# The fill of an attention stage: the chain's slices take precedence over scores, in banks of their own, with rows written from other queues

## The chip, the core and the metric

The kernel runs on one core of one Trainium2 chip. Times are device microseconds (us) of a whole execution. The engines are PE (TensorE; PEld is its weight load), DVE (VectorE), ACT (ScalarE), POOL (GpSimd) and SP (SyncE, which here only issues DMAs). Each engine works through its own instructions in order and waits for others at semaphores.

## What is computed

The reference is a stack of four "macaron" blocks on 2048 rows of 128 numbers, in float32. Each block is half a feed-forward step, attention (or a long convolution), and another half feed-forward step, each on a layernorm of the rows and added to them. The change bears on the last two blocks:

```python
x = x + 0.5 * _L2_ffn_ref(_layernorm(x), ...)   # gate, up, down: 128 -> 384 -> 128
x = x + _L2_attn_ref(_layernorm(x), ...)        # 16 heads of 8, rotary
x = x + 0.5 * _L2_ffn_ref(_layernorm(x), ...)
x = x + 0.5 * _L3_ffn_ref(x, ...)               # gated attention of 16 heads, then experts
x = x + _L3_attn_ref(_layernorm(x), ...)        # 16 heads of 8, rotary, causal
x = x + 0.5 * _L3_ffn_ref(x, ...)
```

So there are four attentions of 16 heads: L2's own (here rope2), that within the first L3 feed-forward step (gated0), L3's own (rope3, causal) and that within the second L3 feed-forward step (gated1).

## The kernel before, in words

**Tiles.** The 2048 rows are four chunks (`NC`) of 512 (`CW`), each four tiles (`TC`) of 128. Keys of all heads lie in `kp`, 128 partitions x 8 pairs of heads x 2048, in a high and a low part with rows of constants between them (ones, `one_rows`), so that a score and the subtraction of its maximum are one matmul. A query unit is one chunk and one group of four heads, (qc, g); `qps` are four buffers for units, with a constant filling of zeros. Two rows of such a buffer take minus the maxima (`h_mT`). Values are in `va`.

**An attention** is the function `attend`. It walks through half-steps: a score step (matmuls `sn` into a bank pair of pool `sc`, two of them, then the DVE reduction `h_mx`) and a weight step (matmuls `st` into pool `tp`, three banks, an exponential on ACT to `pr`, and the products with values, `av`). A unit's weights need all of its maxima: when its last score is out, `maxima` (L1018 on) forms `h_m`, `h_mr`, `h_mt` on DVE, transposes them on PE (`mt_ps`), copies them on ACT (`h_mT`) and writes four DMAs into `qp`.

**Modes.** `order["mode"]` is "fill" while no weight has been issued, "core" from the first weight, and "drain" when the scores are those of the next attention. In fill the attention has nothing but scores of unit 0 (and then of unit 1) and what it is still missing: the chain `carried`, with the last chunk's feed-forward step (`l2_chunk` for rope2: norm, matmuls `gu`, `hid`, `po`, sum into x) and then `prepare` (norm, transposes `xn_tp`, projection `pj`, rotation `rot` with the tables `cos` and `sin`, high and low part, and for keys `spread` into `kp` from on chip, `keys_here`). Beside it runs `own`, with values of all chunks and queries 1 to 3. In each step of the loop both of these are given one slice, so slices and scores alternate.

**What sets the order.** `pin` keeps a PE instruction in program order when `order["pinned"]` is set: scores and weights always, slices in all modes but fill. DVE work of class `Ordered` is kept in order in core, drain and host. What is not kept in order is placed by a scheduler. Buffers of `banks()`, such as `pj` and `gu`, come in fill from pool `sc`, the same as the scores'.

**Keys.** The first three chunks of rope2's keys were written to DRAM (`dk`) during the stage before. `attend` loads them by SP at its start (`load_keys`, in two halves of four pairs, 24 DMAs of 128 KB). Ahead of a load the constants of all rows must be in `kp`: `constant_rows` for pairs 0 to 3 in `head_buffers`, for 4 to 7 in `other_rows()`, called between the halves. Pairs with p % 4 < 2 are written by ACT (L1538), the others by DVE (L1540); `qps` 0 by DVE and 1 to 3 by POOL (L1544), followed by the memset of `va` (L1549).

Of the kernel before, what the change touches and what calls it, by code (L numbers as in the profile page):

```python
# [2 lines left out]

# [1 line left out]

# [6 lines left out]
F32 = mybir.dt.float32  # L12
# [4 lines left out]
ALU = mybir.AluOpType  # L17
# [4 lines left out]
P = 128  # L22
# [3 lines left out]
CW = 512  # L26
NC = S // CW
# [3 lines left out]
HD = 8  # L31
NG = 4
PARK = 2
NEG = -1.0e30
NK = 32
KD = 64
# [7 lines left out]
def tile_macaron(ctx: ExitStack, tc: tile.TileContext, a: dict, out: bass.AP):  # L44
    nc = tc.nc
# [23 lines left out]
    order = {"pinned": False, "mode": "free"}  # L69
# [23 lines left out]
    def transpose(dst, src):  # L93
        pin(nc.tensor.transpose(dst, src, ident))  # L94
# [3 lines left out]
    pools = {"keep": ctx.enter_context(tc.tile_pool(name="keep", bufs=1))}  # L98
# [28 lines left out]
    one_rows = const.tile([P, 1], F32, name="one_rows")  # L127
# [556 lines left out]
            return self.tiles[key[1]][key[0], key[2]]  # L684

    def banks(name):
        if order["mode"] == "host":
            return TwoBanks(name)
        return pools["sc"].tile([P, 2, CW], F32, tag="sc", name=name)

# [17 lines left out]
    def chain(tasks):  # L708
        for task in tasks:
            yield from task  # L710
            yield 1
# [52 lines left out]
    class Heads:  # L764
# [3 lines left out]
        def __init__(self):  # L768
            self.current = False
            self.queries = {}  # L770
            self.units = [(qc, g) for qc in range(NC) for g in range(NG)]
            self.scores, self.weights = [], []
            for u in self.units:
                nk = u[0] + 1 if self.causal else NC
                nkb = (u[0] + 1) * TC if self.causal else NT
                if u == self.units[0]:
                    self.scores += [(self, u, t, kc) for kc in range(nk) for t in range(TC)]
                else:
                    self.scores += [(self, u, t, kc) for t in range(TC) for kc in range(nk)]
                self.weights += [(u, kb) for kb in range(nkb)]  # L780
            self.scored = 0
            self.waiting_keys, self.loaded, self.sent, self.valued, self.ready = [], set(), set(), set(), set()


# [2 lines left out]
        def keys_here(self, c):  # L787
            cs = slice(c * CW, (c + 1) * CW)
            hi, lo = (kp[:, 2 * PARK + n, cs] for n in range(2))
            yield from self.project("k", c, hi, lo)  # L790
# [32 lines left out]
            yield 1  # L823


        def load_keys(self, c, halves=(0, 1)):
            for h in halves:
                ps = slice(4 * h, 4 * h + 4)
                for j in range(2):
                    for n in range(2):  # L830
                        r = j * KD + n * 2 * HD
                        nc.sync.dma_start(
                            out=kp[r : r + 2 * HD, ps, c * CW : (c + 1) * CW].bitcast(F32),
                            in_=rows_of(dk[c], j)[:, ps, :],
                        )
            self.loaded.update((c, h) for h in halves)
# [137 lines left out]
    def attend(A, carried, follow, after=None):  # L974
# [6 lines left out]
        def begin(B, u):  # L981
            qc, g = u
            assert qc in B.sent
            qp = qps[turn["qp"] % len(qps)]
            turn["qp"] += 1
            for j in range(2):
                nc.sync.dma_start(
                    out=qp[j * KD : j * KD + KR + 2, :, :].bitcast(F32),
                    in_=rows_of(dq[qc], j)[:, 2 * g : 2 * g + 2, :],
                )  # L990
            mx = small.tile([P, TC, 4, NC], F32, tag="h_mx", name="h_mx")
            B.queries[u] = qp, mx

        def score(B, u, t, kc, p):
            qc, g = u
            qp, mx = B.queries[u]
            diag = B.causal and kc == qc
            wd = (t + 1) * P if diag else CW
            sc = banks("sn")
            for j in range(2):  # L1000
                r = slice(j * KD, (j + 1) * KD)
                pin(nc.tensor.matmul(  # L1002
                    sc[:, j, :wd], lhsT=qp[r, p, t * P : (t + 1) * P],
                    rhs=kp[r, 2 * g + p, kc * CW : kc * CW + wd], start=True, stop=True,
                ))
            if diag:
                vec.tensor_tensor(
                    sc[:, :, wd - P : wd], sc[:, :, wd - P : wd],
                    mask_qk.unsqueeze(1).to_broadcast([P, 2, P]), ALU.add,
                )  # L1010
            vec.tensor_reduce(mx[:, t, 2 * p : 2 * p + 2, kc], sc[:, :, :wd], AX.X, ALU.max)

        def maxima(u):
            qc, g = u
            qp, mx = queries[u]
            nk = qc + 1 if causal else NC
            m = small.tile([P, TC, 4], F32, tag="h_m", name="h_m")
            vec.tensor_reduce(m, mx[:, :, :, :nk], AX.X, ALU.max, negate=True)  # L1018
            mr = small.tile([P, TC, 4], F32R, tag="h_mr", name="h_mr")
            vec.tensor_copy(mr, m)  # L1020
            mt = small.tile([P, TC, 4, 2], F32, tag="h_mt", name="h_mt")
            vec.tensor_copy(mt[:, :, :, 0], mr.bitcast(F32))
            vec.tensor_tensor(mt[:, :, :, 1], m, mr.bitcast(F32), ALU.subtract)
            yield 1
            pt = bank("mt_ps")[0:8, :]
            for t in range(TC):
                transpose(
                    pt[:, t * P : (t + 1) * P], mt[:, t, :, :].rearrange("p s h -> p (s h)")
                )
            mT = small.tile([8, CW], F32R, tag="h_mT", name="h_mT")  # L1030
            nc.scalar.copy(mT, pt)  # L1031
            for s in range(4):
                r = (s % 2) * KD + KR
                nc.sync.dma_start(
                    out=qp[r : r + 2, s // 2, :].bitcast(F32), in_=mT[2 * s : 2 * s + 2, :].bitcast(F32)
                )

# [72 lines left out]

        if units[0] not in queries:
            begin(A, units[0])
        for h in range(2):
            for c, halves in A.waiting_keys:
                if h in halves:
                    A.load_keys(c, (h,))
            if h == 0 and A is rope2:
                other_rows()
        LAG = 4
        waiting = []  # L1120
        ready = {}
        last = None
        own = chain([A.value(c) for c in range(NC)] + [A.query(c) for c in range(1, NC)])
        beside = [[0, task] for task in (*carried, own)]
        followed = 0

        n = nw = 0
        while nw < len(weights) or last:
            order["pinned"] = True
            B = A if A.scored < len(A.scores) else after  # L1130
            s = B.scores[B.scored] if B and B.scored < len(B.scores) else None
            w = weights[nw] if nw < len(weights) else None
# [17 lines left out]
            k = units.index(s[1]) + 1 if s and B is A else len(units)  # L1150
# [11 lines left out]
            for _, task in due:  # L1162
                later = next(task, None)
                if later is not None:
                    waiting.append((n + later, task))
            if order["mode"] == "drain":
                while followed in finished:
                    beside.append([n, chain(follow(followed))])
                    followed += 1
            order["pinned"] = order["mode"] != "fill"  # L1170
            for entry in beside[:2]:
                if entry[0] <= n:
                    later = next(entry[1], None)
                    if later is None:
                        beside.remove(entry)
                    else:
                        entry[0] = n + later
# [348 lines left out]
    def head_buffers(pool):  # L1526
        kp = pool.tile([P, NH // 2, S], F32R, name="kp")
        va_flat = pool.tile([P, NT, NH * (HD + 1) + 32], F32, name="va")
        qps = [pool.tile([P, 2, CW], F32R, name=f"qp{k}") for k in range(4)]
        n = (NC - 1) * CW  # L1530


        def constant_rows(pairs):
            for p in pairs:
                dst = kp[:, p, 0:n].rearrange("p (t d) -> p t d", d=P)
                src = ones.unsqueeze(1).to_broadcast([P, n // P, P])
                if p % 4 < 2:
                    nc.scalar.activation(dst, src, AF.Identity, bias=one_rows, scale=0.0)  # L1538
                else:
                    nc.vector.tensor_scalar(dst, src, 0.0, one_rows, ALU.mult, ALU.add)  # L1540

        for k, qp in enumerate(qps):
            engine = nc.gpsimd if k else nc.vector
            engine.tensor_scalar(  # L1544
                qp.rearrange("p k (t d) -> p (k t) d", d=P), ones.unsqueeze(1).to_broadcast([P, 2 * TC, P]),
                0.0, None, ALU.mult,
            )
        constant_rows(range(4))
        nc.gpsimd.memset(va_flat, 1.0)  # L1549
        spread_w = pool.tile([P, 2, 2, P], F32R, name="spread_w")  # L1550
        return kp, va_flat, qps, spread_w, lambda: constant_rows(range(4, 8))

    with early:
# [4 lines left out]
        with tc.tile_pool(name="act1", bufs=1) as act:  # L1558
# [10 lines left out]
            rope2, rope3 = RopeHeads("l2", w2, False), RopeHeads("l3", w3, True)  # L1569
            l1_ffn(w1, [chain([l2_chunk(c, w2), rope2.prepare(c)]) for c in range(NC - 1)])  # L1570
    heads = ctx.enter_context(tc.tile_pool(name="heads", bufs=1))
    kp, va_flat, qps, spread_w, other_rows = head_buffers(heads)
# [134 lines left out]
```

## Time and profile before

| | us |
|---|---|
| runs (three) | 4069.31, 4070.45, 4085.0 |
| median | 4070.45 |
| profiled execution, its own time | 4069.46 |
| its span | 4067.7 |
| PE busy | 3575.4 (88%) |
| DVE busy | 3120.2 (77%) |
| ACT busy | 2378.7 (58%) |
| POOL busy | 279.1 (7%) |

The mean granted clock of TensorE was 0.888. The fills of the four attentions, found in the trace by the last x of the chain and the first `st`:

| attention | fill, about us | first norm's result on PE | first st |
|---|---|---|---|
| rope2 | 737 to 852 | 755.78 | 852.27 |
| gated0 | 1573 to 1665 | 1589.47 | 1665.23 |
| rope3 | 2505 to 2592 | | 2592.31 |
| gated1 | 3163 to 3210 | 3179.90 | 3209.87 |

Busy shares are averages over these fills and the long core and drain stages between, so they are read by stretches, as below. In a row of a view, "out<-in" names the tiles, "x4" the number of instructions, and an arrow in a wait points to what ended it.

### The profile page before, as it was taken

How to read it: one execution, taken by the hardware profiler on the slowest of the kernel's cores; microseconds unless marked ns; L12 is line 12 of the kernel's file. 1: busy time of each engine (PE TensorE's matmuls, PEld its weight loads, DVE VectorE, ACT ScalarE, POOL GpSimd, SP SyncE). 2: the span in 40 equal slices, each digit the busy share in tenths (PEclk: the TensorE clock that was granted, in tenths of full speed). 3: DMA queues.
4: the chain of work that ended last, by engine and by line, in shares of the span. 5: the costliest groups of instructions: out<-in, count | busy, mean ns of one | idle time of the engine just before them, and what ended most of it. 6: DMA issues, size and time to landing. Idle time of an engine off the chain costs nothing. (4 is left out here: it accounts for less than half of the span.)

```text
span 4067.7 us, 72222 instructions
## 1 busy us (share of the span) xinstructions
PE 3575.4 (88%) x29160; PEld 1695.2 (42%) x29160; DVE 3120.2 (77%) x5432; ACT 2378.7 (58%) x4515; POOL 279.1 (7%) x528
## 2 busy tenths in 40 slices
PE   8789899589999996899999965589997899999965
PEld 8556655333333342333333343233333333333334
DVE  2855354589999974799999845489996799999844
ACT  1222133168888862688888722246675588888732
POOL 2000011210000000000000023100000000000013
PEclk9889799789999997899999966578897899999965
DMA  2100000210000001100000022300002100000012
GB/s 71 24 1 1 1 16 27 52 53 7 10 7 10 5 12 42 35 7 10 7 10 5 9 63 76 97 24 11 10 2 57 44 10 7 10 7 7 7 46 71
DMA packets 63630, 98.96 MB, mean 24 GB/s; under 512 B 8656, under 2 KB 28864, under 8 KB 63040
## 3 DMA queue, kind: packets, MB, share of 16 engines
q1 hardware_dynamic: 54224, 70.86, 6.3%
q0 software_dynamic: 7728, 22.91, 2.1%
q8 instruction: 230, 3.77, 0.4%
q14 instruction: 104, 0.85, 0.1%
q10 hardware_dynamic: 1344, 0.57, 0.1%
HBM read 64.25 MB, written 29.00 MB: 23 GB/s over the span
## 5 line engine op out<-in xcount | busy, mean ns | idle before, releaser
L84 DVE TENSOR_REDUCE h_mx<-sn 128x2 f32<-128x1024 f32 (+1 forms) x1856 | 2204.6, 1197 | 133.9 <-PE sn L1002 111.9
L1058 ACT ACTIVATE pr<-st 128x512 f32<-128x512 f32 x3712 | 1971.3, 585 | 512.8 <-PE st L76 322.2
L76 PE MATMUL av<-pr,va 128*32 128x256 f32 x14592 | 1188.4, 398 | 10.8 <-ACT h_ot L1087 10.7
L76 PE MATMUL st<-qp,kp 64*128 64x512 f32 x3712 | 996.2, 499 | 43.9 <-ACT pr L1058 38.9
L1002 PE MATMUL sn<-kp,qp 64*128 64x512 f32 (+3 forms) x3712 | 804.9, 413 | 104.3 <-DMA qp<-dq 58.5
L76 PEld LDWEIGHTS st<-qp,kp 64*128 64x128 f32 x3712 | 394.7, 188 | 809.5 <-ACT pr L1058 427.7
L76 PEld LDWEIGHTS av<-pr,va 128*32 128x32 f32 x14592 | 292.6, 109 | 662.6 <-issue 625.5
L1002 PEld LDWEIGHTS sn<-kp,qp 64*128 64x128 f32 x3712 | 385.3, 194 | 165.3 <-issue 64.0
L614 ACT ACTIVATE hid<-h 128x512 f32<-128x512 f32 x128 | 76.2, 597 | 235.2 <-PE h L76 229.5
L84 DVE TENSOR_TENSOR hid<-hid,h 128x512 f32<-128x512 f32 x128 | 87.3, 686 | 114.3 <-PE h L76 102.3
L76 PEld LDWEIGHTS po<-w_l_w3T,hid 128*128 128x128 f32 x1024 | 126.5, 193 | 38.4 <-issue 28.0
L76 PE MATMUL po<-w_l_w3T,hid 128*128 128x128 f32 x1024 | 128.6, 278 | 4.8 <-DVE hid L84 4.7
L76 PE MATMUL h<-m_xc,w_l_w12T 128*128 128x512 f32 x256 | 128.5, 640 | 0.1
L1392 POOL DMA_INDIRECT wt<-in_b_wt,w_row_i x30 | 28.6, 953 | 1434.8 <-DVE slot_i L84 1387.3
L76 PE MATMUL h<-xnT,w_l_w12T 128*128 128x512 f32 x256 | 118.1, 604 | 0.4 <-DVE logits L594 0.4
L247 POOL TENSOR_TENSOR x<-x,w_b_n2b 128x512 f32<-128x512 f32 x8 | 10.1, 1266 | 1130.9 <-DVE rows L84 1127.4
L84 DVE BATCH_NORM_STATS2 st<-ph 128x6 f32<-128x256 f32 x46 | 19.9, 432 | 88.0 <-PE ph L76 88.0
L94 PE MATMUL xn_tp<-ident,xn_t 128*128 128x128 f32 x64 | 20.5, 401 | 75.2 <-ACT xn_t L213 71.7
L1031 ACT CAST h_mT<-mt_ps 8x512 fp32r<-8x512 f32 x64 | 36.8, 575 | 80.7 <-PE mt_ps L94 80.5
L84 DVE TENSOR_TENSOR st<-st,mask_kq 128x128 f32<-128x128 f32 x256 | 63.2, 290 | 17.6 <-PE st L76 16.8
L84 DVE TENSOR_TENSOR sn<-sn,mask_qk 128x256 f32<-128x256 f32 x128 | 54.0, 425 | 27.8 <-PE sn L1002 26.5
L76 PEld LDWEIGHTS h<-m_xc,w_l_w12T 128*128 128x128 f32 x256 | 50.3, 207 | 51.5 <-issue 48.2
(420 smaller groups left out, 2863.1 us busy)
## 6 DMA issues: line engine op xcount, KB each, us to landing
qp<-dq SPq DMA_DIRECT2D x128, 136.0 KB
kp<-dk SPq DMA_DIRECT2D x88, 128.0 KB
dq<-hi SPq DMA_DIRECT2D x32, 256.0 KB
dq<-lo SPq DMA_DIRECT2D x32, 256.0 KB
wt<-in_b_wt SPq DMA_DIRECT2D x16, 258.0 KB
qp<-h_mT SPq DMA_DIRECT2D x256, 4.0 KB
cos<-in_l_cos POOLq DMA_DIRECT2D x12, 256.0 KB, 4.0
sin<-in_l_sin POOLq DMA_DIRECT2D x12, 256.0 KB, 5.2
```

What stands on the lines that cost most here:

```text
L76: pin(nc.tensor.matmul(dst, lhsT=lhsT, rhs=rhs, start=start, stop=stop))
L84: ins = method(*args, **kw)
L94: pin(nc.tensor.transpose(dst, src, ident))
L247: nc.gpsimd.tensor_tensor(xs, xs, row.unsqueeze(1).to_broadcast([P, TC, D]), ALU.add)
L614: nc.scalar.activation(hid[:, hb, :], p_1, AF.Silu)
L1002: pin(nc.tensor.matmul(sc[:, j, :wd], lhsT=qp[r, p, t * P : (t + 1) * P], rhs=kp[r, 2 * g + p, kc * CW : kc * CW + wd], start=True, stop=True,
L1031: nc.scalar.copy(mT, pt)
L1058: nc.scalar.activation(pr[:, off:CW], sc[:, off:], AF.Exp, scale=A.scale)
L1392: nc.gpsimd.indirect_dma_start(wts[k], None, a["b3_wt"], bass.IndirectOffsetOnAxis(ap=w_row_i[:, s - E : s - E + 1], axis=0),)
```

## The change

- In fill, `banks()` gives two single banks of pool `tp`; scores take theirs from `sc` directly in all modes.
- In fill nothing on PE is kept in program order, scores included. A slice of the chain (not of `own`) is emitted at a higher priority (`AHEAD`, 2000) for the scheduler.
- Queries 1 to 3 leave `own` and become `asking`, started once all scores of unit 0 are out (`A.first`).
- The rows of maxima (`h_mT`) are written from POOL's queue in fill and from SP's otherwise.
- For rope2 the second halves of the keys (`late_keys`), with their constants (`other_rows()`), wait until the mode is no longer fill, and are loaded from POOL's queue.
- Constants: pairs 0 and 1 by ACT, 2 and 3 by DVE, 4 to 7 by POOL and kept in order; all four `qps` by DVE.

```diff
     def banks(name):
-        if order["mode"] == "host":
+        if order["mode"] in ("host", "fill"):
             return TwoBanks(name)
...
+            self.first = sum(score[1] == self.units[0] for score in self.scores)
...
-        def load_keys(self, c, halves=(0, 1)):
+        def load_keys(self, c, halves=(0, 1), queue=nc.sync):
...
-                        nc.sync.dma_start(
+                        queue.dma_start(
...
-            sc = banks("sn")
+            sc = pools["sc"].tile([P, 2, CW], F32, tag="sc", name="sn")
...
-                nc.sync.dma_start(
+                where = nc.gpsimd if order["mode"] == "fill" else nc.sync
+                where.dma_start(
                     out=qp[r : r + 2, s // 2, :].bitcast(F32), in_=mT[2 * s : 2 * s + 2, :].bitcast(F32)
                 )
...
+        late_keys = []
         for h in range(2):
             for c, halves in A.waiting_keys:
-                if h in halves:
+                if h and A is rope2:
+                    late_keys.append(c)
+                elif h in halves:
                     A.load_keys(c, (h,))
-            if h == 0 and A is rope2:
-                other_rows()
...
-        own = chain([A.value(c) for c in range(NC)] + [A.query(c) for c in range(1, NC)])
+        own = chain([A.value(c) for c in range(NC)])
+        asking = [chain([A.query(c) for c in range(1, NC)])]
...
-            order["pinned"] = True
+            order["pinned"] = nw > 0
...
-            order["pinned"] = order["mode"] != "fill"
+            if order["mode"] != "fill" and late_keys:
+                other_rows()
+                for c in late_keys:
+                    A.load_keys(c, (1,), nc.gpsimd)
+                late_keys.clear()
+            if asking and A.scored >= A.first:
+                beside.append([n, asking.pop()])
             for entry in beside[:2]:
                 if entry[0] <= n:
-                    later = next(entry[1], None)
+                    ahead = order["mode"] == "fill" and entry[1] is not own
+                    with tc.high_priority(offset=AHEAD) if ahead else nullcontext():
+                        later = next(entry[1], None)
...
-                if p % 4 < 2:
+                if p < 2:
                     nc.scalar.activation(dst, src, AF.Identity, bias=one_rows, scale=0.0)
+                elif p < 4:
+                    nc.vector.tensor_scalar(dst, src, 0.0, one_rows, ALU.mult, ALU.add)
                 else:
-                    nc.vector.tensor_scalar(dst, src, 0.0, one_rows, ALU.mult, ALU.add)
+                    tc.keep_in_program_order(
+                        nc.gpsimd.tensor_scalar(dst, src, 0.0, one_rows, ALU.mult, ALU.add)
+                    )
...
         for k, qp in enumerate(qps):
-            engine = nc.gpsimd if k else nc.vector
-            engine.tensor_scalar(
+            nc.vector.tensor_scalar(
                 qp.rearrange("p k (t d) -> p (k t) d", d=P), ones.unsqueeze(1).to_broadcast([P, 2 * TC, P]),
                 0.0, None, ALU.mult,
             )
```

More of the change, by code (lines that the diff above doesn't have):

```diff
@@ L1 @@
 import math
-from contextlib import ExitStack
+from contextlib import ExitStack, nullcontext
 import numpy as np
@@ L33 @@
 PARK = 2
+AHEAD = 2000
 NEG = -1.0e30
```

## The prediction

> **What bounds the kernel now.** I read the page's first part, then the engine windows, then the waits of one window, then single tiles. The first part says that PE is busy for 88% and DVE for 77%, which hides that the kernel has stages with different limits. The windows (busy us of each engine in a stretch, instructions in brackets, then the granted TensorE clock, DMA share, GB/s) tell them apart:
>
> ```profile
> 750.00:800.00 50.00, 30.34 (x96) 15.48 (x96) 27.89 (x33) 4.02 (x8) 3.96 (x17) 0.70 0.31 68
> 800.00:850.00 50.00, 34.00 (x86) 14.43 (x86) 30.48 (x42) 9.71 (x17) 15.78 (x28) 0.62 0.25 78
> 900.00:950.00 50.00, 49.76 (x484) 18.67 (x484) 49.01 (x47) 43.33 (x81) 0.00 (x0) 1.00 0.02 8
> 1600.00:1650.00 50.00, 37.17 (x128) 19.90 (x128) 20.65 (x30) 17.15 (x29) 4.04 (x15) 0.70 0.00 0
> 2540.00:2590.00 50.00, 13.72 (x55) 9.15 (x55) 19.26 (x44) 5.17 (x9) 11.28 (x23) 0.53 0.52 124
> ```
>
> In 900 to 950, a core stage, PE (49.76) and DVE (49.01) are both full at clock 1.00: nothing can be hidden there, and what stops DVE there is lost for good. The other four rows are fill stages: no engine is full and the clock is 0.53 to 0.70. There a chain of dependent steps sets the end. The waits of the first fill (rope2, 738 to 853) name it (total us waited, times, longest):
>
> ```profile
> POOL ln_h L185 <- DVE ln_g L84: 48.9, 2, 47.6
> ACT xn_t L213 <- POOL ln_nb L208: 27.1, 2, 21.4
> POOL rot L902 <- DVE rot L84: 22.8, 3, 10.0
> PEld xn_tp L94 <- ACT xn_t L213: 22.5, 6, 16.2
> PE xn_tp L94 <- ACT xn_t L213: 21.0, 2, 16.0
> DVE h_mx L84 <- PE sn L1002: 19.0, 6, 5.8
> DVE va L84 <- POOL va L1549: 4.0, 1, 4.0
> ```
>
> PE waits 16.0 us for the first norm, and POOL 47.6 for statistics that stand behind scores on DVE. The change works in these fills: rope2 about 115 us long, gated0 93, rope3 88, gated1 48. It can gain only there, and whatever it pushes out of a fill goes into a full core stage.
>
> **Rope2's fill, by steps.** Times are those of the profiled run. Two tiles price the constants (ns min/median/max, first and last start):
>
> ```profile
> L1544 POOL TENSOR_SCALAR qp<-ones x3: 3470/3471/3488, 737.3 to 744.2; 128x1024 fp32r<-128x1024 f32 x3
> L1544 DVE TENSOR_SCALAR qp<-ones x1: 680/680/680, 738.3 to 738.3; 128x1024 fp32r<-128x1024 f32 x1
> L1538 ACT ACTIVATE kp<-ones,one_rows x4: 1562/1562/1577, 737.2 to 741.6; 128x1536 fp32r<-128x1536 f32 x4
> L1540 DVE TENSOR_SCALAR kp<-ones,one_rows x4: 1012/1780/1819, 738.9 to 743.2; 128x1536 fp32r<-128x1536 f32 x4
> ```
>
> *Start.* x of chunk 3 is ready at 738.3. POOL's three qp constants (10.4) and the memset of va (2.4) hold DVE up until 750.07 (the 4.0 above); ln_g comes at 750.9, POOL's 14 small operations take 3.9, xn_t ends at 755.2. After: DVE makes four qp (4 x 0.68) and two kp (2 x 1.01) constants, 4.7 us, with the statistics among them: ln_g at 742.5, xn_t at 746.6, **8.6 us earlier**.
>
> *Chain before scores.* The order of the built kernel puts the six gate and up groups of matmuls and po ahead of the scores. Before, they stood among scores from 768.8 and x was ready at 794.57. Three pairs at 3.9 (half clock) are 12; with xn_tp, xc and po, x is ready at 767. The second norm takes 6 (before, four h_mx stood ahead of it: POOL began only at 804.45), pj of key and query ends at 779.4 (before 817.3): **38 us earlier**.
>
> *Scores behind it.* Of unit 0's 32 h_mx, 29 now come after rot: 29 x 1.14 = 33, rot 0.7, some 5 idle for the spread keys: the last at 819 (before 838.8). So 38 becomes **20**; PE, with 29 score pairs and 16 spread matmuls at half clock (29 x 0.99 + 16 x 0.5 = 37), is nearly as long, so that no more is likely.
>
> *To the first weight.* Before, from the last h_mx to the first st: 838.8 to 852.27, 13.5 us. After, two h_mx (2.3) stand among the h_m steps, and the pj pair of query 1 (3.8 at half clock) among mt_ps; the four row DMAs go through POOL, whose cos issue (0.56) is shorter than SP's 0.75 per row but which does rot and lo (1.26 each) between them. I take 19.5: first st at 838.5, **-14 us** (from -6, if PE binds, to -22).
>
> *Queries.* Query 2 and 3 were done in this fill; now in the core: one pj pair at half clock, 3.8, and one at full, 1.9: **+6**.
>
> *The late keys.* This is the dearest step. In POOL's order after query 2's lo stand: four kp constants of 128x1536, cos of query 3, twelve kp loads, sin of query 3, then rot and lo. DVE, in order, has query 3's rot after only six h_mx of the core, and it needs cos and sin. All later h_mx are behind it; they free the two score banks, PE's next scores wait for these, and the weights behind them on PE too. Counted from the first st: lo ends at +10. The constant on POOL is not in the trace at this size; the nearest row is 3.47 for 1024, so 5.2 for 1536, 20.8 for four: +31. cos +0.6; twelve issues at 0.6 (cos, of the same order of bytes) are 7; SP's 24 loads of 128 KB took 26.95 us, 1.12 each, so that twelve take 13.5, and sin, issued last, lands behind them after its own 5: about +49. DVE comes to the rot at +15 (six h_mx, two rot, a little wait). Loss **34**, plus about 1 of clock on restart.
>
> Here a rule and a row part. The Trainium skill, "GPSIMD Engine Reference", section 4.1, says that GpSimd's elementwise work with one input is roughly at line rate. By that the four constants would cost about what DVE's cost alone, 4 x 1.01 = 4, and the stall 34 - 17 = 17. The rows above have the same operation and shape on both engines: 3.47 on POOL, 0.68 on DVE, five times. I take the row. Bounds for one constant: 1.0 and, if its second operator costs another pass, 10.4.
>
> **The other fills.**
> - *Gated0.* Chunk 2's norm begins after one h_mx and not four (3 x 1.15 = 3.5), gate and up one score earlier, po about 5.6 earlier; its second norm still has h_mx ahead. One q_ps and sg_ps move to the core (2). **-4** (-11 to +3).
> - *Rope3.* PE waits 17.9 for unit 1's query, with mt_ps queued behind, until 2580.45; mt_ps 2583.74, first st 2592.31. After, mt_ps stands straight behind unit 0's scores (2566), the rows go through a POOL idle until 2598.97: first st near 2579, 13 earlier. But unit 1's scores still can't begin before 2580.45 and are then among weights. **-8** (-13 to -3).
> - *Gated1.* Queries leave a short fill and two h_mx get in the way: **0** (-2 to +2).
>
> **Edits at nothing.** Separate banks: fill's scores keep their two banks and the chain gets its own; the transposes share three, no wait seen. spread_in stands first on SP: its copy waited 5.6 us on ACT, which works only 22 of the 116 us from 737 to 853. Unit 1's rows stand behind query 3's writes on SP: under 2 us, inside the stall; without it they'd be bare.
>
> **Sum.** -14 + 6 + 34 + 1 - 4 - 8 = **+15** against the profiled run's 4069.46 (span 4067.7, 1.8 around it), which is 1 below the median of 4070.45: 4085.
>
> **Rivals.**
> 1. *Chance 0.57: the sum as it stands*, 4070 to 4102.
> 2. *Chance 0.23, slower: the POOL constant is dearer.* It has two operators and a pointer operand where the row has one and none. At 10.4 each the late keys cost 21 more: 4106. From 6.7 each the result is beyond 0.5%. For it: POOL's share is that of slow, plain work. Against it: DVE's price per element is the same for one operator and two (0.66 ns).
> 3. *Chance 0.20, faster: no long stall.* At 1.0 each and with the loads running quicker in an otherwise idle DMA system, the stall is about 15; then -14 - 4 - 8 + 6 + 16 gives 4066, and with the fills at their better ends (-22, -9, -12) 4048. For it: the core's DMA share is 0.02. Against it: the measured 3.47.
> 4. *The precedence is real* in the order of instructions; that it is ignored is no case. That PE at half clock eats the fill's gain is in the bound of -6: 4093.
>
> **Chances.** 0.5% is 20 us, about what a measurement of this kernel can tell from no change. Faster (below 4050): 0.16, from rival 3. Within: 0.33 of case 1, 0.03 of 2, 0.04 of 3: 0.40. Slower (above 4091): 0.24 of case 1 and 0.20 of 2: 0.44. The range, 4048 to 4110, holds case 1 and most of 2 and reaches rival 3's better end; case 1's own is 4070 to 4102.
>
> **What would show it.** In the changed profile: ln_g at about 742 and x of chunk 3 at 767; first st near 838; POOL's kp constants at 5.2 each; then an idle time of DVE of some 30 us before rot, released by a DMA of sin, with PE idle and the clock down just after the fill; first st of rope3 13 us after mt_ps. If POOL's constants are near 1.5 us, or if DVE's rot comes without a wait, the forecast is wrong on the fast side; if they are over 7, or if rope2's first st comes no earlier than 846, on the slow side.

## The result and the profile after

| | us |
|---|---|
| before, median of 13 runs | 4070.45 (4062.35 to 4085.0) |
| after, median of 13 runs | 4087.47 (4079.53 to 4097.37) |
| ratio after to before, 95% interval | 1.0039 [1.0027, 1.0051] |
| profiled execution, span before and after | 4067.7 and 4083.0 |

The kernel became 17.0 us slower, 15.3 in the profiled execution. Forecast were 4085 and +15. The head of the page after the change:

```profile
span 4083.0 us, 72225 instructions
...
PE 3604.4 (88%) x29160; PEld 1715.9 (42%) x29160; DVE 3119.9 (76%) x5433; ACT 2375.8 (58%) x4513; POOL 292.1 (7%) x557
```

PE is busy 29.0 us longer with the same 29160 matmuls (the mean granted clock was 0.883 for 0.888), and DVE is not busy longer at all: nothing was added on DVE, it waits more. The waits of rope2's fill and of the core's beginning (738 to 900) say where:

```profile
POOL ln_h L186 <- DVE ln_g L85: 19.8, 2, 17.8
ACT xn_t L214 <- POOL ln_nb L209: 15.8, 2, 10.9
...
PE xn_tp L95 <- ACT xn_t L214: 14.1, 2, 7.6
...
PE sn L1004 <- DVE rot L85: 13.1, 1, 13.1
...
DVE rot L85 <- PE pj L77: 12.5, 6, 8.2
...
DVE rot L85 <- DMA sin<-in_l_sin: 9.4, 1, 9.4
...
PE st L77 <- DMA qp<-h_mT: 5.7, 1, 5.7
```

The chain's waits of before have shrunk: PE waits 7.6 for the first norm (16.0 before), POOL 17.8 for statistics (47.6). New are DVE's wait for sin and PE's behind it. The timeline shows them in place (start, length, engine, idle time before it and what ended that):

```profile
843.95 6.13 POOL L1556 TENSOR_SCALAR kp<-ones,one_rows 128x1536 fp32r<-128x1536 f32 x4
...
850.03 0.64 POOL L883 DMA_DIRECT2D cos<-in_l_cos  x1
850.67 4.68 POOL L834 DMA_DIRECT2D kp<-dk  x9
...
853.88 0.75 DVE L85 SCALAR_TENSOR_TENSOR rot<-pj,w_l_bcol,cos 128x512 f32<-128x512 f32 x1 [5.04 <-DMA cos<-in_l_cos]
...
858.09 0.56 POOL L883 DMA_DIRECT2D sin<-in_l_sin  x1 [0.30 <-DMA kp<-dk]
...
864.06 0.75 DVE L85 SCALAR_TENSOR_TENSOR rot<-pj,w_l_bcol,sin 128x512 f32<-128x512 f32 x1 [9.42 <-DMA sin<-in_l_sin]
...
864.86 0.79 PE L1004 MATMUL sn<-kp,qp 64*128 64x512 f32 x2 [13.13 <-DVE rot L85]
```

The chain reads from top to bottom: four constants, then cos, then twelve key loads, then sin, all in POOL's order; DVE sits 5.04 + 9.42 = 14.5 us before the two halves of query 3's rot, and PE's next score 13.1. But the four constants take 6.1 us together, not 20.8.

**By stage.** In the trace each of the 64 units closes with one copy on ACT (`h_ot`). Inside the core stages of rope2, gated0 and gated1 these copies keep their distance to 0.6 us or better from one kernel to the next (the last one or two of a stage to 1); in rope3 they wander by several us, so its core is counted in its column. The difference of their start times, each kernel minus before, therefore splits the time (us; the last column is the span's). The second column is the part of the first that is already there when the fill begins, at the end of chunk 3's first x (738.36 before). The first copies, before and after, from which the +1.3 is taken:

```profile
896.62 0.59 ACT L1087 COPY h_ot<-av 128x512 f32<-128x512 f32 x1
897.94 0.59 ACT L1090 COPY h_ot<-av 128x512 f32<-128x512 f32 x1
```


| kernel | rope2's first unit | of it ahead of the fill | gated0's fill | experts and rope3 | gated1's fill | whole |
|---|---|---|---|---|---|---|
| after | +1.3 | +0.2 | -3.1 | +4.2 | +8.2 | +15.3 |
| late keys after query 3 | -12.6 | -0.1 | -2.7 | +4.0 | +8.3 | +0.9 |
| rows by SP | +2.9 | +2.0 | +4.4 | -6.7 | +5.2 | +9.3 |
| queries in own list | -18.3 | -2.4 | -4.0 | -7.0 | +3.2 | -22.1 |
| no precedence | -2.5 | -0.4 | -11.3 | -1.2 | -0.2 | -8.7 |
| queries in own list, no precedence | -18.1 | +1.7 | -11.1 | -0.1 | +0.6 | -25.9 |
| the same, second profile | -17.8 | +2.0 | -11.1 | -3.3 | +0.5 | -27.5 |
| and rows by SP | -9.2 | +2.3 | -8.7 | +3.4 | +0.0 | -10.3 |
| and shared banks | +6.7 | +3.4 | +0.3 | +0.2 | +0.4 | +8.3 |
| and old constants | -15.7 | -0.7 | -8.6 | -6.9 | +3.6 | -28.2 |
| and old constants, two of POOL's in another form | -13.4 | +1.6 | -8.9 | -12.6 | +0.0 | -34.6 |
| and priority, scores in order | -10.4 | +5.4 | -4.0 | +1.9 | +0.7 | -7.7 |
| before, with separate banks alone | -14.0 | -0.9 | -10.3 | -6.8 | +0.0 | -27.8 |

What is left of the whole lies in the core stages (about 1 each) and behind the last unit, where every kernel but two ends 1.5 to 4.4 later than that one profile of before: that follows no edit.

How far one profile can be trusted is seen where kernels are the same. What lies ahead of rope2's fill shifts by 2.3 between the two kernels with old constants, so rope2 is best read from the fill's beginning (first column less the second): the best kernel then stands at -19.8 in both of its profiles, and both kernels with old constants at -15.0. In gated1 these last two, which have the same code there, differ by 3.6, and 3.5 of that lies ahead of the unit's maxima; so a difference of 3 in one profile is not firm unless the trace shows its place. The column of experts and rope3 can't be read finer than some 6: those two differ by 5.7 in it.

### The profile page after: what moved, and what is told of

Its sections match the earlier page's. It is cut to its first block, busy times and chain, and to the rows that moved or that the text cites. A ratio compares the mean times of both kernels' runs of the same rounds, so it can differ in the third digit from the quotient of the medians.

```text
span 4083.0 us, 72225 instructions
## 1 busy us (share of the span) xinstructions
PE 3604.4 (88%) x29160; PEld 1715.9 (42%) x29160; DVE 3119.9 (76%) x5433; ACT 2375.8 (58%) x4513; POOL 292.1 (7%) x557
## 4 chain that ended last, share of the span: by engine, by line
PE 75%; DVE 11%; issue 4%; ACT 4%; DMA 3%; POOL 3%; SPq 0%; POOLq 0%; ACTq 0%; DVEq 0%
PE av L77 23%; PE st L77 18%; PE sn L1004 9%; PE po L77 6%; PE h L77 5%; DVE h_mx L85 4%; ACT pr L1061 2%; PE ph L77 2%; DVE st L85 1%; PE gu L77 1%; PE km L77 1%; PE ot_ps L95 1%; DVE ln_stats L85 1%; PE kv L77 1%; PE mt_ps L95 1%
## 5 line engine op out<-in xcount | busy, mean ns | idle before, releaser
L1004 PE MATMUL sn<-kp,qp 64*128 64x512 f32 (+3 forms) x3712 | 825.0, 419 | 105.7 <-DVE h_mx L85 43.8
L1004 PEld LDWEIGHTS sn<-kp,qp 64*128 64x128 f32 x3712 | 394.5, 196 | 166.6 <-DVE h_mx L85 64.6
L77 PEld LDWEIGHTS po<-w_l_w3T,hid 128*128 128x128 f32 x1024 | 126.6, 194 | 38.4 <-issue 28.2
L85 DVE TENSOR_TENSOR st<-st,mask_kq 128x128 f32<-128x128 f32 x256 | 63.4, 291 | 19.5 <-PE st L77 18.9
L77 PEld LDWEIGHTS h<-xnT,w_l_w12T 128*128 128x128 f32 x256 | 47.1, 195 | 47.5 <-issue 46.3
```

Source lines behind the costliest of these rows:

```text
L77: pin(nc.tensor.matmul(dst, lhsT=lhsT, rhs=rhs, start=start, stop=stop))
L85: ins = method(*args, **kw)
L1004: pin(nc.tensor.matmul(sc[:, j, :wd], lhsT=qp[r, p, t * P : (t + 1) * P], rhs=kp[r, 2 * g + p, kc * CW : kc * CW + wd], start=True, stop=True,
```

## The experiments

Each group of kernels ran on one chip, beside the kernel before. Edits are against the changed kernel where nothing else is said. A kernel of which one time is given was timed once, in the profiled execution: its stages can be read, its total only roughly.

**The late keys alone.**

```diff
-            if order["mode"] != "fill" and late_keys:
+            if NC - 1 in A.sent and late_keys:
```

> Changed kernel, but rope2's late keys (their constants on POOL and their twelve loads) are issued only after query 3 has been sent. Theory A (the late keys in POOL's queue cost the core two idle times of DVE, 5.0 us for cos and 9.4 us for sin, and nothing hides them): rope2's first unit closes 14 us earlier than in the changed kernel, some 13 us ahead of the kernel before, and the whole time falls by as much, to about 4073 us. Rival B (most of that idle time only brings forward a wait for the late keys or for query 3 that would come anyway): the first unit closes at most 5 us earlier and the time stays above 4080 us.

Measured: 4067.61 against 4067.41 before, ratio 0.9996 [0.9979, 1.0013]. rope2's first unit closes 13.9 earlier than in the changed kernel. The same stretch of DVE:

```profile
847.64 1.23 DVE L85 TENSOR_REDUCE h_mx<-sn 128x2 f32<-128x1024 f32 x1
850.17 0.75 DVE L85 SCALAR_TENSOR_TENSOR rot<-pj,w_l_bcol,cos 128x512 f32<-128x512 f32 x1 [1.31 <-PE pj L77]
850.84 0.74 DVE L85 SCALAR_TENSOR_TENSOR rot<-pj,w_l_bcol,sin 128x512 f32<-128x512 f32 x1
851.50 3.48 DVE L85 TENSOR_REDUCE h_mx<-sn 128x2 f32<-128x1024 f32 x3
```

Up to 847.6 it is the same to 0.1 us; then rot waits 1.3 for PE instead of 14.5 for tables, and h_mx goes on 13.2 us earlier. Theory A holds in rope2: nothing hid the stall. No other stage of the table moved by more than 0.4, so it is the whole difference between slower and no change. The absolute time of theory A, 4073, was too high: this chip's before was 3 lower as well.

**The rows of maxima back on SP's queue.**

```diff
-                where = nc.gpsimd if order["mode"] == "fill" else nc.sync
-                where.dma_start(
+                nc.sync.dma_start(
```

> Changed kernel, but the rows of maxima (h_mT) go through SP's queue in fill, as before. Theory A (in POOL's queue the rows stand behind rot, lo, cos and sin of the queries, which is why the second pair of st waits 5.7 us in rope2 and 3.4 us in gated1): rope2's first unit closes 3 us earlier and gated1's first unit loses 4 us less against the kernel before (4 us in place of 8). Rival B (SP's queue has the writes of the queries, which wait for hi and lo as well): no stage moves by more than 2 us, or rope2's gets later.

One time: 4079.04. gated1 loses 5.2 in place of 8.2, so 3 of theory A's 4 are there, but rope2 closes no earlier (from its fill's beginning, 0.9 for 1.2). The wait for the rows in rope2 stays, 5.73 us before the second st from POOL's queue and 6.15 before the second pair from SP's; theory A is wrong there. gated0's fill came out 7.5 longer, and all of it lies ahead of the rows' DMAs (counted from the unit before, mt_ps starts 7.6 later), so this profile doesn't price the rows in gated0. In gated1 up to the first st the two kernels agree to 0.1 us, so that the 3 are those of the rows. But it is not what theory A had in mind, other work in POOL's order. First the changed kernel, then the rows by SP:

```profile
3213.93 1.59 POOL L1037 DMA_DIRECT2D qp<-h_mT  x3 [28.07 <-ACT h_mT L1033]
...
3218.44 0.50 POOL L1037 DMA_DIRECT2D qp<-h_mT  x1 [2.92 <-issue]
...
3220.73 1.19 PE L77 MATMUL st<-qp,kp 64*128 64x512 f32 x3 [3.41 <-DMA qp<-h_mT]
...
3211.72 2.68 SPq L1036 DMA_DIRECT2D qp<-h_mT  x4
```

From POOL three of the four rows go out at once, the fourth after 2.9 us in which POOL does nothing, and PE's fourth st waits 3.4 for it; SP sends all four without a gap. The gap is not other work of POOL. It stands in gated1 of all eight profiles in which rope2's late keys are loaded from POOL's queue and the rows written from it, and in neither of the two in which the rows alone are (four at once in 2.08). So it goes with what was moved to POOL's queue in a stage long past, the loads or their constants; what holds the fourth row up is open.

**Queries 1 to 3 in the list of values.**

```diff
-        own = chain([A.value(c) for c in range(NC)])
-        asking = [chain([A.query(c) for c in range(1, NC)])]
+        own = chain([A.value(c) for c in range(NC)] + [A.query(c) for c in range(1, NC)])
+        asking = []
```

> Changed kernel, but queries 1 to 3 stand behind the values in their list again and so begin in the fill. Theory A (the queries that were pushed out of a short fill into a full core cost gated1 and rope3 their time): gated1's first unit loses 3 us or less against the kernel before (8 in the changed kernel) and rope3 ends 4 us earlier than in the changed kernel; rope2's long stall goes too, since query 3 is projected ahead of the late keys (12 us or more). Rival B (the loss of gated1 is that of scores that are no longer in order): gated1 keeps its 8 us.

One time: 4047.36. rope2's first unit closes 19.6 earlier than in the changed kernel (17.1 from the fill's beginning): the stall of 14.5 is gone, as query 3 is projected in the fill, and the core has no projections left. gated1 loses 3.2 and not 8.2. Theory A in both, in gated1 at the edge of its 3; rival B is not excluded for what remains. Its third claim, rope3 4 earlier (-7.0 for +4.2), lies in the column that is too coarse for it.

**No precedence.**

```diff
-            order["pinned"] = nw > 0
+            order["pinned"] = True
...
+            order["pinned"] = order["mode"] != "fill"
             for entry in beside[:2]:
...
-                    ahead = order["mode"] == "fill" and entry[1] is not own
+                    ahead = False
```

> Changed kernel, but scores in fill are kept in program order and slices of the chain have no higher priority, as before; banks, queries, rows and late keys stay as changed. Theory A (precedence is what shortens rope2's fill): rope2's first weight comes 10 us or more later than in the changed kernel and its first unit closes 10 us or more later. Rival B (the earlier constants on DVE and the separate banks are what shortens it): at most 5 us later. For gated1, rival B of the third run expects its 8 us of loss to go here.

One time: 4060.76. In rope2 x is ready at 773.6 (763.9 with precedence, 794.6 before), and yet unit 0's maxima are formed at 819.3 for 817.8: ten us on the chain are worth 1.5 at the end of the fill. The changed kernel first, then that without precedence:

```profile
763.90 0.69 DVE L85 SCALAR_TENSOR_TENSOR x<-po,x 128x512 f32<-128x512 f32 x1 [2.69 <-PE po L77]
817.84 0.21 DVE L85 TENSOR_REDUCE h_m<-h_mx 128x16 f32<-128x64 f32 x1
...
773.58 0.68 DVE L85 SCALAR_TENSOR_TENSOR x<-po,x 128x512 f32<-128x512 f32 x1
819.27 0.20 DVE L85 TENSOR_REDUCE h_m<-h_mx 128x16 f32<-128x64 f32 x1
```

Its first unit even closes 3.8 earlier; gated0's fill is 8.2 shorter, and gated1's loss of 8.2 is gone altogether. So the precedence, the change's first part, costs time. Rival B holds for rope2, and gated1 does as the third run's rival B expected. A reading of this, not tested apart: chain and scores share DVE and PE, and what goes first on the chain goes last for the reductions.

Two parts of the change each remove gated1's loss or most of it when undone, scores that are not kept in order (loose scores) and late queries, so it is a product of both. In the trace of the changed kernel it builds up in steps, counted from the unit before: 2.3 at the maxima; 3.7 at mt_ps, where query 1's projection lands among the transposes (mt_ps spans 3210.30 to 3213.03, 2.7 us, where before it took 1.0); 3.4 at the first av; 8.2 at the unit's close. The last 4.8 lie in the core, where the projections of queries 2 and 3 now stand: matmuls q_ps and sg_ps of 5.9 us by their own durations between the first av and the close, where before there were 1.3.

**Both undone.**

> Changed kernel with queries 1 to 3 in the list of values again and without the precedence (scores in order, no higher priority); banks, rows, constants and late keys as changed. Theory A (two separate costs: the postponed queries cost rope2's stall, and loose scores with a preferred chain cost the two gated fills): the two gains of the single runs add, rope2's first unit 18 us ahead of the kernel before, gated0's fill 11, gated1's 0, and the time is about 4035 us. Rival B (the two edits remedy the same thing): no more than the 22 us of the run with queries in the fill, so about 4047 us or above.

4036.39 against 4071.49, ratio 0.9917 [0.9887, 0.9947]. By stage the two gains add (-18.1 and -11.1), as theory A said. This is faster than both kernels.

**With the rows by SP.**

> The kernel of the run before (queries in the list of values, no precedence) with the rows of maxima on SP's queue. Theory A (with queries out of the tail of the fill neither queue has anything ahead of the rows): every stage within 2 us of the run before. Rival B (POOL's queue is what keeps the rows off SP's writes of queries): rope2 or a gated fill 4 us or more later.

4044.83 (4029.79 to 4059.62), ratio 0.9933 [0.9909, 0.9956]. The intervals overlap. Its profiled execution took 4059.62, 15 over its median, so that its stages are weak evidence (rope2 8.9 later, which would be rival B; but 4.8 of 8.2, counted from the fill's beginning, are there before the maxima are formed, ahead of any row). Not settled.

**With shared banks.**

```diff
-        if order["mode"] in ("host", "fill"):
+        if order["mode"] == "host":
...
-            sc = pools["sc"].tile([P, 2, CW], F32, tag="sc", name="sn")
+            sc = banks("sn")
```

> The kernel with queries in the list of values and no precedence, and with chain slices and scores in one pool of two bank pairs in fill, as before. Theory A (fill is bound by the reductions on DVE, which free a pair each in 1.2 us, so that the chain has to wait for a score's pair at each of its matmuls): rope2's first unit 4 to 10 us later than with separate banks. Rival B (banks are never short): all stages within 2 us.

One time: 4077.76. rope2's first unit closes 24.8 later (23.1 from the fill's beginning) and gated0's fill is 11.4 longer than with separate banks. Theory A said 4 to 10: right in kind, short by more than half. The waits of 740 to 828, first with separate banks:

```profile
POOL ln_h L186 <- DVE ln_g L85: 31.7, 2, 25.3
...
PEld sn L1004 <- DVE h_mx L85: 20.1, 19, 3.7
...
ACT hid L746 <- PE gu L77: 8.0, 3, 3.6
```

and with shared ones:

```profile
POOL ln_h L186 <- DVE ln_g L85: 60.6, 2, 54.2
ACT hid L746 <- PE gu L77: 32.9, 3, 20.0
```

With shared banks ACT waits up to 20.0 for a pair of gate and up matmuls (3.6 with separate ones), and POOL 54.2 for the second norm's statistics: each slice takes its place in the row of scores, whose pairs come free at DVE's pace.

**With the old constants and loads.** The edits of the last hunks of the change, of `late_keys` and of `other_rows()` are undone.

> The kernel with queries in the list of values and no precedence, and with constants and key loads as before (POOL's three query buffers at 3.47 us, four constants each on ACT and DVE, all key loads by SP ahead of the fill). Theory A (the first norm waits for these): xn_tp starts 8 us later and rope2's first unit closes 8 us or more later than with the new constants. Rival B (scores on DVE set the end of the fill and take up the 8 us): less than 3 us later.

One time: 4041.25. rope2's first unit closes 2.4 later, but this profile's fill also began 2.4 earlier: counted from the fill's beginning it closes 4.8 later (-15.0 for -19.8, and each of the two numbers was found in two profiles). The first norm's result on PE comes 5.3 later by the same count, and not 8: 12.2 after x for 17.4. The new constants first, then the old:

```profile
752.24 0.86 PE L95 MATMUL xn_tp<-ident,xn_t 128*128 128x128 f32 x2 [10.76 <-ACT xn_t L214]
...
755.08 0.86 PE L95 MATMUL xn_tp<-ident,xn_t 128*128 128x128 f32 x2 [16.04 <-ACT xn_t L214]
```

Neither theory, then. What makes the 4.8 isn't settled: the norm is 5.3 earlier, but the loads were moved as well, and in the last run below, with POOL's old constants in a quicker form, the norm is 1.7 earlier than here and the unit closes no earlier. The 8.6 of the forecast are there only with the precedence (9.0 after x in the changed kernel), where DVE takes the statistics among the constants.

**Priority alone, scores in order** (the kernel with queries in the list of values, with the first two hunks of "No precedence" and not the third).

> The same kernel with the higher priority of the chain's slices, but with the scores still in program order. Theory A (the loose scores are what costs: the projections and rows slip between reductions only where scores may move): as without any precedence within 2 us in each fill (gated0's 11 ahead, gated1's 1 behind). Rival B (the priority costs by itself, as it delays values and scores behind the chain's slices): gated0's fill only 4 ahead and gated1's 3 behind, as in the run with queries in the fill and full precedence.

One time: 4061.72. gated0's fill gains 4.0 and not 11.1, as rival B said: the priority by itself costs its 7 us. gated1's is 0.7, as theory A said: there the loose scores cost (0.7 for 3.2, one profile each). Each theory holds in one fill.

**Separate banks alone**, on the kernel before (there `banks()` and `sn` take the two lines that "With shared banks" removes).

> The kernel before with one part of the change alone: separate banks in fill. Theory A (the banks are what is worth anything; without them the run with the other parts lost 25 us of rope2's gain): rope2's first unit 12 to 18 us ahead of the kernel before, gated0's fill some 9 to 11 shorter, and a time of about 4042 us, equal within 8 us to the run with all parts but the precedence and the postponed queries. Rival B (the banks help only where the earlier constants have started the chain early): at most 8 us in all, 4062 us or above.

4046.49 against 4072.16, ratio 0.9943 [0.9924, 0.9962]: -14.0 in rope2, -10.3 in gated0. Theory A. Beside it the best kernel again:

> The kernel with queries in the list of values and without the precedence, timed again beside the kernel before with separate banks alone. Theory A: about 4036 us, as in its first three rounds, and up to 8 us faster than the banks alone, by the earlier constants. Rival B: the same as the banks alone within 3 us, the constants being hidden behind the scores.

4041.08, ratio 0.9922 [0.9895, 0.9950]. The intervals overlap, so what the other parts add to the banks is seen in the stages only: in rope2, from the fill's beginning, -19.8 for -13.1, of which the constants and loads make 4.8.

**The price of a constant on POOL.** On the kernel with old constants:

```diff
-            engine.tensor_scalar(dst, src, 0.0, None, ALU.mult)
+            if k == 2:
+                engine.tensor_scalar(dst, src, 0.0, 0.0, ALU.mult, ALU.add)
+            elif k == 3:
+                engine.tensor_scalar(dst, src, 0.0, one_rows, ALU.mult, ALU.mult)
+            else:
+                engine.tensor_scalar(dst, src, 0.0, None, ALU.mult)
```

> To price the POOL constant: the kernel with old constants, separate banks, queries in the list of values and no precedence, where the three query buffers that POOL fills take three forms of one operation at the same size (128x1024): one operator (0.0, as before), two operators with two numbers, and two operators with a number and a pointer (zero times the row column, so the value is zero in all). Theory A (the form sets the price: the kp constant has two operators and a pointer, and cost 1.00 ns per element where the one-operator row cost 3.39): the third takes 1.03 us, the first 3.47. Rival B (the place sets it: at the start of the fill other engines write as well): all three take about 3.5 us.

The tile's rows (ns min/median/max, then start):

```profile
L1565 POOL TENSOR_SCALAR qp<-ones x1: 3491/3491/3491, 738.9 to 738.9; 128x1024 fp32r<-128x1024 f32 x1
L1561 POOL TENSOR_SCALAR qp<-ones x1: 1742/1742/1742, 742.3 to 742.3; 128x1024 fp32r<-128x1024 f32 x1
L1563 POOL TENSOR_SCALAR qp<-ones,one_rows x1: 1798/1798/1798, 744.1 to 744.1; 128x1024 fp32r<-128x1024 f32 x1
```

The time was 4034.86 beside 4062.52 for before, one of each. Neither theory as it stood. The one-operator form costs twice the two-operator forms, at the same place and size; in the kernel before it takes 3.47 even for the third buffer (from 744.2), when DVE's constants are almost done. But 1.80 for 1024 is still more per element (1.76 ns) than the late constants' 1.54 for 1536 (1.00 ns). What differs is the neighbour: beside the two-operator rows DVE was writing its own constants of 1536, and one of these took 4.26 us, where it takes 1.01 alone:

```profile
L1554 DVE TENSOR_SCALAR kp<-ones,one_rows x4: 1014/1789/4257, 740.4 to 744.8; 128x1536 fp32r<-128x1536 f32 x4
```

The late constants ran beside reductions of scores or an idle DVE. The changed kernel shows the same from POOL's side: one small operation of a norm takes 0.85 beside DVE's constants and 0.20 two us later, behind them.

```profile
742.03 0.85 POOL L187 TENSOR_TENSOR ln_h<-ln_h,ln_v 128x4 f32<-128x4 f32 x1
744.45 0.20 POOL L187 TENSOR_TENSOR ln_h<-ln_h,ln_v 128x4 f32<-128x4 f32 x1
```

So the two engines seem to hinder each other while DVE writes its constants; how much of the 1.80 that makes, and how much the shape, no run isolates.

## Why the prediction was right, and where it was not

The total was right, 4085 for 4087, and so was the mechanism of its largest term: the late keys in POOL's queue stop DVE at query 3's rot, and with them out of the way the change is worth nothing either way (0.9996). That the total came within 3 us is luck all the same: this term was put 21 us too high, and losses that were not forecast, in gated1 and rope3 above all, made up for it. The forecast's own sign of being wrong on the fast side, POOL's constants near 1.5 us, did show, at 1.54.

| term | forecast | measured |
|---|---|---|
| rope2, start of weights | -14 | -15.0 (first av 840.8 for 855.9); the first st itself came 24.1 earlier, 828.21, and the next waited 5.7 for its rows |
| late keys and clock | +35 | +13.9 (without them -12.6, with them +1.3) |
| queries 2 and 3 in the core | +6 | about +2.4 (from -15.0 to -12.6, without the stall) |
| gated0 | -4 | -3.1 |
| rope3 | -8 | +4.2, with the experts; not firm |
| gated1 | 0 | +8.2 |
| the rest | 0 | +4.7, of it 2.9 behind the last unit, where most kernels show as much |

- **The step that was mis-sized is "The late keys".** The term "5.2 for 1536, 20.8 for four" measured 1.54 and 6.1. The row it was scaled from, qp on POOL, was the same size class and operation name but has one operator; the run on forms shows that form to be twice as dear as those with two. Here the rule that I had weighed and left was nearer: "GPSIMD Engine Reference", section 4.1, of the Trainium skill puts work with one input at roughly line rate, and POOL's 1.54 stands against DVE's 1.01 (L1553 in the changed kernel): 1.5 times, not five. The rest of the term was nearer: from the first load's issue (850.67) to the rot that waits for sin (864.06) are 13.4 us, where the forecast's steps from +31.6 to +49 gave 17.4. The two together are 18.7 of the 19.5 by which the stall of 34 came out shorter, 14.5.
- **The faster rival's price was the nearer one**, 1.0 for 1.54, and its stall of about 15 came. Still its time of 4066 did not come, since gated1 and rope3 gave nothing. (Its better end takes -9 and -12 for gated0 and rope3, where their own ranges went to -11 and -13: 4045 and not 4048.)
- **gated1 was put at 0** with "two h_mx get in the way". These were there, with the late query among mt_ps and a fourth row 2.9 late. The larger part, 4.8, is queries 2 and 3 in the core: for rope2 they had been priced at +6, for gated1 at nothing, though it is the forecast's own rule that what leaves a fill goes into a full core stage.
- **rope3: -8.** The first st came 8.4 earlier (2583.93 for 2592.31), as forecast in kind, but the unit's scores began 9.8 later (2564.10 for 2554.29), and nothing of the gain was left at the end of the stage. Of these 9.8, 9.4 are there at the first transpose of rope3's norm (2518.74 for 2509.32), behind the experts. There PE's clock was granted 0.77 before and 0.57 after (before first in each pair):

```profile
2509.32 1.63 PE L94 MATMUL xn_tp<-ident,xn_t 128*128 128x128 f32 x4 [30.16 <-ACT xn_t L213]
2518.74 1.63 PE L95 MATMUL xn_tp<-ident,xn_t 128*128 128x128 f32 x4 [30.58 <-ACT xn_t L214]
...
2450.00:2500.00 50.00, 26.32 (x119) 18.30 (x119) 23.71 (x89) 11.83 (x30) 19.62 (x21) 0.77 0.28 73
2450.00:2500.00 50.00, 35.54 (x118) 26.01 (x117) 19.13 (x66) 10.19 (x26) 12.26 (x14) 0.57 0.25 64
```

  Counted from the core ahead, that transpose comes 2.7 to 11.6 later than in this one profile of before in every other profile on record, with separate banks alone 9.4. From 60 to 130 us behind that core the clock was 0.71 before, 0.67 with rows by SP (2.7 later), and 0.60 to 0.62 in the other profiles read for it (6.0 to 11.6 later). So the shift goes with the clock of that one profile of before and not with an edit of rope3; what sets the clock there is open. Counted from the transpose the first unit closes 9.3 earlier, near the forecast, but with separate banks alone it is 10.5, so that this doesn't show the forecast's step.
- **"Edits at nothing" held the most valuable edit.** The separate banks were put down as seeing "no wait"; alone they make the kernel before 0.9943 of its time. The wait was in the profile of before: POOL's 47.6, and ACT's for the gate and up matmuls that stood among scores (738 to 853):

```profile
ACT hid L745 <- PE gu L76: 27.1, 3, 14.5
```

  I booked its end to the chain's precedence. The run without precedence shows that the precedence brings x ten us forward and the fill's end 1.5.
- **The rival that PE or DVE take up the fill's gain** was right as the bound it was given: 38 us on the chain became 20 at the last maximum, in forecast (819) and trace (817.8).

## What to carry to other kernels

A transfer or constant that is moved to an idle engine's queue is late for whatever follows it in that queue: look for the next instruction there that a full engine waits for, and price the whole stretch. When a chain and a bulk of independent work share buffers, give each its own before changing their order; here the order on top of that brought the chain ten us forward and the end of the fill 1.5. A total that comes out right is no proof of its terms: measure them by stage, and against a second profile where a stage differs by a few us.

## What the runs showed of the hardware

On POOL a tensor_scalar of 128x1024 with one operator took 3.47 to 3.49 us, and with two operators 1.74 (numbers) or 1.80 (a pointer) at the same place; with two operators at 128x1536, beside DVE's reductions or an idle DVE, 1.54. On DVE one operator at 1024 took 0.68 and two at 1536 1.01. DVE's constants of 1536 took up to 1.82 each at the start of before's fill while POOL wrote too, once 4.26 in the run on forms, and 1.01 in the changed kernel beside POOL's small operations, which then took up to 0.85 in place of 0.20. Four row DMAs issued from POOL in gated1 had a gap of 2.9 us before the fourth, with POOL idle, in the eight profiles whose late keys had been loaded from POOL, and none in the two others; from SP there was none. The clock granted in the same 50 us of the experts was 0.77 in one profile and 0.57 in another.
